# A planned graph-network kernel: cap turned by DMA, heads in twos, full products in layer three, GRU update on VectorE

## Chip, cores, metric

The kernel runs on one core of a Trainium2 chip. The metric is device time in microseconds of one launch. Engines are named as the profile names them: PE (TensorE matmuls), PEld (its weight loads), DVE (VectorE), ACT (ScalarE), POOL (GpSimd), SP (the queue that issues most DMAs).

## The reference

There are 64 graphs of 256 nodes with 256 features, `x`, and a 0/1 adjacency `adj`, which is about 1.6% full. Four layers follow one another; each takes h = relu(layernorm(x)) and adds its result to x.

- Layers 0 and 1: attention with 4 heads of 64. Scores e[i,j] = leaky_relu(src[i] + dst[j]) where there is an edge, softmax over j, product with the projected features Wh. (In layer 1 the edge types are 1 to 5, of which a 0/1 adjacency has type 1 alone.) Layer 0 ends in ELU; layer 1 adds a bias, relu, Wh, and a layer norm of each head.
- Layer 2: the same attention with one head of 256.
- Layer 3: three GRU steps. In each, m = h W_i, ag = A^T m, and

```
r = sigmoid(i_r + h_r);  z = sigmoid(i_z + h_z)
n = tanh(i_n + r * h_n)
h = (1 - z) * n + z * h
```

with i = ag w_ih^T + b_ih and h_* = h w_hh^T + b_hh.

## The kernel before

The work goes by pairs of graphs, 32 of them: a tile has 128 partitions, and `C` = 4 chunks of 128 nodes make the two graphs, `S` = 512 columns.

**The order.** A class `_Schedule` plans it while the program is built. Each piece of work is an `op` with an engine, a cost in ns, what it reads and writes, and the buffers that it takes. Due times are set backwards from `PACE` ns for each pair, with `STRETCH` times the cost and `MARGIN` between a piece and its user. Then a simulated clock runs, and each engine takes the enabled piece that is due first and has room in its buffers. The order found is laid down as the fixed order of every engine. Pieces of two or three neighbouring pairs thus interleave on each engine. Buffers are slots by name: 5 `xt`, 1 `at`, 3 `cap`, 1 `cap_n`, 3 `pt`, 9 `g`, 8 PSUM banks, and so on. An engine works in its order and waits where its next piece is not yet ready. The planner knows nothing of the chip beyond these costs.

**Softmax without a running maximum.** exp(leaky_relu(s + d)), up to a factor of the row, is the larger of two products of one column factor and one row factor. `factors` makes the factors: `f` (of the rows on partitions) by two ACT exponentials, and `cb`, the other factor repeated over all partitions. `cb` is made in one of two ways: for the first `SPREAD_PAIRS` = 2 pairs by broadcast matmuls (`spread`, L1075), later by a transpose (L1094), a small DMA to DRAM (`rd`) and a DMA that repeats it into SBUF. `weights` (L1128, then a minimum with `cap` on L823) gives the unnormalised weights `pt` on DVE: four `tensor_scalar` pieces and one `tensor_tensor`. `cap` is 2^120 where there is an edge, and 0 elsewhere; a row without any edge gets 2^-80 throughout.

**cap.** `layer0` loads `at` (the adjacency as int32). ACT takes a Square that checks that the values are 0 or 1 (L1191). DVE sums the degrees (L1197) and makes them 2^-80 or 0 (L1198). POOL casts `at` to bf16 `am`, and makes `cap_n` from it in four pieces (L1205). PE turns the eight 128x128 blocks (`turn`, L1218), and ACT copies them from PSUM to `cap`.

**attend.** A product of weights and features takes `pt` as the stationary operand in two halves of 64 columns:

```python
Q = P // 2
for jc in range(2):
    for q in range(2):
        i0 = ic * P + q * Q
        nc.tensor.matmul(ps[q * Q : (q + 1) * Q], lhsT=pt.tile[:, b, jc, i0 : i0 + Q], ...)
```

The profile shows these on L1148 as 128*64: 32 matmul records a head in layers 0 and 1 (65 columns, the last one the row sum), and 32 a pair in layer 2 (257 columns). `attend_head` does one head as one piece of PE work.

**GRU.** `gru` first splits h into a rounded part and the rest (`split`, `hl`), so that A^T h can be had in the faster fp32r form (`aggregate`, L1345). The W_i are folded into the input weights beforehand (`wc`). `gate` (L1359) makes the gate products in full fp32: 128x512, of `whh` with `ht` and of `wc` with `ag`. Each step has two units of 128 features; `unit` computes sigmoid as 0.5 (1 + tanh(v / 2)):

```python
d = ht - n                     # POOL
d = (z + 1) * d                # DVE, z is the tanh
h_new = 0.5 * d + n            # DVE
```

`rows_of` (L1373) turns h_new by PE for the next step, or for the sum onto `xt` at the end. A line L823 in the profile is the helper `vec`, through which most DVE, ACT and POOL pieces go; they are told apart by their tiles.

Of the kernel before, what the change touches and what calls it, by code (L numbers as in the profile page):

```python
# [518 lines left out]
SPREAD_PAIRS = 2  # L519
PACE = 97000.0  # L520
# [19 lines left out]
class _Schedule:  # L540
# [16 lines left out]
    STRETCH = 3.17  # L557
    MARGIN = 400.0
# [166 lines left out]
def _fast_path(  # L725
# [38 lines left out]
    P = 128  # L764
# [3 lines left out]
    NP = B // 2  # L768
# [16 lines left out]
    viol = consts.tile([P, NP + 1], F32, name="viol")  # L785
# [21 lines left out]
            "cb4_": (slots, 2), "cb1_": (slots, 1), "pt": (slots, 3), "o": (slots, 2),  # L807
# [106 lines left out]
    def check_columns():  # L914
# [4 lines left out]
        def norms():  # L919
# [12 lines left out]
        vec(nc.vector.tensor_scalar, 100, viol[:, NP : NP + 1], lambda: fit.tile[:, :1], -1.0, 1.0,  # L932
            op0=OP.mult, op1=OP.add, reads=[fit], writes=[(B_viol, NP)])
# [36 lines left out]
    def parts(b, keys):  # L970
        return [(b, k) for k in keys]

    def norm(xt, cls):

        st, mv = buf("st", [P, C, 6]), buf("mv", [P, 4, C])
        xn = buf(cls, [P, C, D])

        def stats(c):
            def emit():
                nc.vector.bn_stats(st.tile[:, c, :], xt.tile[:, c, :])  # L980
                nc.vector.bn_aggr(mv.tile[:, 0:2, c], st.tile[:, c, :])  # L981

            op("dve", 615, emit, [(xt, c)], [(st, c), (mv, c)])

        for c in range(C):
            stats(c)

        def power():
            nc.gpsimd.tensor_scalar(mv.tile[:, 2, :], mv.tile[:, 1, :], 1e-5, None, op0=OP.add)  # L989
            nc.gpsimd.tensor_tensor(mv.tile[:, 2, :], mv.tile[:, 2, :], nhalf[:, :C], op=OP.pow)  # L990

        op("pool", 1350, power, parts(mv, range(C)), [(mv, "r")])
        vec(nc.vector.scalar_tensor_tensor, 160, lambda: mv.tile[:, 3, :], lambda: mv.tile[:, 0, :], -1.0,
            lambda: mv.tile[:, 2, :], op0=OP.mult, op1=OP.mult,
            reads=parts(mv, range(C)) + [(mv, "r")], writes=[(mv, "b")])

        def apply(c):
            op("act", 610, lambda: nc.scalar.activation(  # L998
                xn.tile[:, c, :], xt.tile[:, c, :], AF.Relu,
                bias=mv.tile[:, 3, c : c + 1], scale=mv.tile[:, 2, c : c + 1],  # L1000
            ), [(xt, c), (mv, "r"), (mv, "b")], [(xn, c)])

        for c in range(C):
            apply(c)
        return xn

    def transposed(xn, cls):
        ht = buf(cls, [P, DC, S])

        def block(dc):  # L1010
            ps = bank()

            def emit():
                for c in range(C):
                    nc.tensor.transpose(  # L1015
                        ps.tile[:, c * P : (c + 1) * P], xn.tile[:, c, dc * P : (dc + 1) * P], ident
                    )

            op("pe", 445, emit, [xn], [ps], takes=[ht])
            vec(nc.scalar.copy, 600, lambda: ht.tile[:, dc, :], lambda: ps.tile,  # L1020
                reads=[ps], writes=[(ht, dc)], engine="act")

        for dc in range(DC):
            block(dc)
        return ht

    def project(ht, we, B_we, heads, width, shift):

        W = width + 2
        wh = buf("wh", [P, heads, C, W])  # L1030

        def rows(c):
            ps = bank()

            def emit():
                for dc in range(DC):
                    nc.tensor.matmul(  # L1037
                        ps.tile[:, : heads * W],
                        lhsT=ht.tile[:, dc, c * P : (c + 1) * P],
                        rhs=we[:, dc].rearrange("p h w -> p (h w)"),  # L1040
                        start=(dc == 0),
                        stop=(dc == DC - 1),
                    )

            op("pe", 895, emit, [ht, B_we], [ps], takes=[wh])

            def copy():
                src = ps.tile[:, : heads * W].rearrange("p (h w) -> p h w", h=heads)
                if shift:
                    nc.scalar.activation(wh.tile[:, :, c, :], src, AF.Identity, bias=shift)  # L1050
                else:
                    nc.scalar.copy(wh.tile[:, :, c, :], src)

            op("act", 390, copy, [ps], [(wh, c)])

        for c in range(C):
            rows(c)
        return wh

    def factors(wh, heads, width, slope, shift):  # L1060

        f = buf("f", [P, 2, heads, C])
        R = heads * C
        cb = buf(f"cb{heads}_", [P, heads, C, P])

        def spread(h):

            ps = bank()

            def emit():
                for c in range(C):
                    nc.tensor.matmul(  # L1075
                        ps.tile[:, c * P : (c + 1) * P],
                        lhsT=wh.tile[:, h, c, width + 1 : width + 2].to_broadcast([P, P]),
                        rhs=ident, start=True, stop=True,
                    )

            op("pe", 880, emit, [wh], [ps], takes=[cb])
            op("act", 700, lambda: nc.scalar.activation(
                cb.tile[:, h].rearrange("p c n -> p (c n)"), ps.tile, AF.Exp,
                scale=slope - 1.0, bias=-shift * (slope - 1.0),
            ), [ps], [(cb, h)])

        if sched.group < SPREAD_PAIRS:
            for h in range(heads):
                spread(h)
        else:  # L1090
            ps, row, rd = bank(), buf("row", [R, P]), buf("rd", [R, P])

            def emit_t():
                nc.tensor.transpose(  # L1094
                    ps.tile[:R, :P], wh.tile.rearrange("p h c w -> p (h c) w")[:, :, width + 1], ident
                )

            op("pe", 115, emit_t, [wh], [ps])

            def emit_row():  # L1100
                nc.scalar.activation(
                    row.tile, ps.tile[:R, :P], AF.Exp, scale=slope - 1.0, bias=-shift * (slope - 1.0)
                )

            op("act", 260, emit_row, [ps], [row])
            dma("act", 1 << 13, lambda: nc.scalar.dma_start(rd.tile, row.tile), [row], [rd])
            dma("sp", heads << 18, lambda: nc.sync.dma_start(
                cb.tile.rearrange("p h c n -> p (h c n)"),
                rd.tile.rearrange("(o r) n -> o (r n)", o=1).to_broadcast([P, R * P]),
            ), [rd], parts(cb, range(heads)))  # L1110

        def exps(k, a):
            op("act", 225, lambda: nc.scalar.activation(  # L1113
                f.tile[:, k], wh.tile[:, :, :, width], AF.Exp, scale=a, bias=-shift * a
            ), [wh], [(f, k)])

        exps(0, 1.0)
        exps(1, slope)
        op("pool", 150, lambda: nc.gpsimd.memset(wh.tile[:, :, :, width], 1.0), [], [wh])  # L1119
        return f, cb  # L1120

    def weights(cap, f, cb, h):

        pt = buf("pt", [P, 2, 2, N])

        def emit(b, jc):
            c = 2 * b + jc
            nc.vector.tensor_scalar(  # L1128
                pt.tile[:, b, jc, :].rearrange("p (i n) -> p i n", n=P),
                cb.tile[:, h, 2 * b : 2 * b + 2, :],  # L1130
                f.tile[:, 1, h, c : c + 1], f.tile[:, 0, h, c : c + 1], op0=OP.mult, op1=OP.max,
            )

        for b in range(2):
            for jc in range(2):
                op("dve", 425, lambda b=b, jc=jc: emit(b, jc), [(cb, h), f], [(pt, (b, jc))], port=True)
        vec(nc.vector.tensor_tensor, 1240, lambda: pt.tile, lambda: pt.tile, lambda: cap.tile, op=OP.min,
            reads=[cap], writes=[pt], port=True)
        return pt

    def attend(ps, pt, wh, c, h, w):
        b, ic = divmod(c, 2)

        Q = P // 2
        for jc in range(2):
            for q in range(2):
                i0 = ic * P + q * Q
                nc.tensor.matmul(  # L1148
                    ps[q * Q : (q + 1) * Q], lhsT=pt.tile[:, b, jc, i0 : i0 + Q],
                    rhs=wh.tile[:, h, 2 * b + jc, :w], start=(jc == 0), stop=(jc == 1),  # L1150
                )

    def attend_head(o, o_view, pt, wh, h):
        ps = bank()
        w = E + 1

        def emit():
            for c in range(C):
                attend(ps.tile[:, c * w : (c + 1) * w], pt, wh, c, h, w)
# [18 lines left out]
    def layer0(pair, p):  # L1178
# [31 lines left out]
        for c in range(C):  # L1210
            capped(c)
# [297 lines left out]
```

## Time and profile before

| | |
|---|---|
| time, median of 3 runs | 3250.36 us (3250.15 to 3252.92) |
| the profiled execution's own time | 3251.65 us |
| its span, first to last instruction | 3249.8 us |
| mean granted TensorE clock | 0.995 |
| gate matmuls, L1359 | 2304 of `whh` and 2304 of `wc`, 128x512 each |
| small head products, L1148, 128x65 | 8192 records, 274.2 us |
| POOL `g<-ht,g` (the d above) | 192, mean 1345 ns |
| DVE `g<-g,g` in the GRU | 384, mean 806 ns |
| DVE degree sums, L1197 | 32, mean 1200 ns |
| ACT copy of cap | 32, mean 1036 ns |

A row of the profile's list of groups has the line, engine and operation, the tiles (out<-in), shapes and count, then the sum of the busy times, the mean of one in ns, and the idle time of the engine just before them with what ended it. The durations of PE's rows overlap, since matmuls are pipelined: what one costs is read as the distance between starts. Shares of the span are averages; the first 200 us and the last 150 us look different from the middle.

### The profile page before, as it was taken

The page shows a single profiled execution, that of the slowest core. Times are in us where ns is not written, and L with a number is a line of the kernel's source. Part 1 is how long each engine was busy: PE and PEld are TensorE (multiplying, and loading weights), DVE is VectorE, ACT ScalarE, POOL GpSimd, SP SyncE. Part 2 cuts the span into 40 slices and gives each one's busy share as a digit, 9 for nine tenths or more (in the row PEclk, how much of TensorE's full clock was granted, in tenths as well). Part 3 has the DMA queues.
Part 4 walks back from the last instruction along what each step waited for, and adds up shares of the span by engine and source line. Part 5 has one row for each costly group of instructions (what it writes and reads, how often), then busy time and mean ns, then how long its engine had stood idle before and what let it go on. Part 6 is the DMA issues. An engine that isn't in the chain of part 4 may idle for free.

```text
span 3249.8 us, 49723 instructions
## 1 busy us (share of the span) xinstructions
PE 3189.6 (98%) x19256; PEld 1901.5 (59%) x19256; DVE 2463.4 (76%) x4965; ACT 1468.8 (45%) x2847; POOL 1131.6 (35%) x1108
## 2 busy tenths in 40 slices
PE   7799999999999999999999999999999999999998
PEld 6556556556656566555565555565565666565554
DVE  8867777787787777787777787877877877777742
ACT  4444444444444444444444444444444454444432
POOL 3532343442343423334332333423434233333220
PEclk9899999999999999999999999999999999999999
DMA  3101111111101101111011111111011011010000
GB/s 100 40 20 43 43 30 46 43 37 43 56 30 40 40 33 56 30 46 43 24 56 43 43 43 34 37 43 56 30 46 42 25 56 40 30 47 21 30 10 14
DMA packets 72549, 129.28 MB, mean 40 GB/s; under 512 B 7736, under 2 KB 60400, under 8 KB 64624
## 3 DMA queue, kind: packets, MB, share of 16 engines
q1 hardware_dynamic: 68368, 124.66, 11.7%
q8 instruction: 154, 2.52, 0.3%
q10 hardware_dynamic: 3936, 1.35, 0.2%
q14 instruction: 91, 0.75, 0.1%
HBM read 108.66 MB, written 17.33 MB: 39 GB/s over the span
## 4 chain that ended last, share of the span: by engine, by line
PE 90%; DVE 7%; POOL 2%; ACT 0%; issue 0%; DMA 0%; ACTq 0%; POOLq 0%; DVEq 0%
PE bank L1359 57%; PE bank L1148 11%; PE bank L1037 10%; PE bank L1345 5%; PE bank L1015 3%; PE bank L1373 2%; DVE pt L1128 2%; DVE st L980 1%; POOL cap_n L1205 1%; DVE mv L981 1%; DVE pt L823 1%; DVE xt L823 0%; PE bank L943 0%; PE bank L1075 0%; DVE mv L823 0%
## 5 line engine op out<-in xcount | busy, mean ns | idle before, releaser
L1359 PE MATMUL bank<-ht,whh 128*128 128x512 f32 x2304 | 1069.0, 596 | 0.4 <-ACT ht L823 0.3
L1359 PE MATMUL bank<-ag,wc 128*128 128x512 f32 x2304 | 1063.0, 594 | 0.0
L1359 PEld LDWEIGHTS bank<-ag,wc 128*128 128x128 f32 x2304 | 424.5, 190 | 482.0 <-issue 476.7
L1359 PEld LDWEIGHTS bank<-ht,whh 128*128 128x128 f32 x2304 | 421.3, 190 | 471.4 <-issue 430.2
L823 ACT ACTIVATE g<-bank,bg 128x512 f32<-128x512 f32 x576 | 393.7, 686 | 573.5 <-PE bank L1359 549.6
L823 DVE SCALAR_TENSOR_TENSOR g<-g,g 128x512 f32<-128x512 f32 x384 | 308.4, 806 | 427.9 <-ACT g L823 424.3
L1128 DVE TENSOR_SCALAR pt<-cb,f 128x256 f32<-128x256 f32 x1152 | 463.4, 470 | 11.0 <-PE bank L1148 8.1
L1148 PEld LDWEIGHTS bank<-wh,pt 128*64 128x64 f32 x9216 | 324.3, 137 | 136.9 <-issue 67.7
L1148 PE MATMUL bank<-wh,pt 128*64 128x65 f32 x9216 | 392.2, 241 | 10.3 <-DVE pt L823 10.3
L823 POOL TENSOR_TENSOR g<-ht,g 128x512 f32<-128x512 f32 x192 | 257.0, 1345 | 290.0 <-ACT g L823 289.9
L823 DVE TENSOR_TENSOR pt<-pt,cap 128x1024 f32<-128x1024 f32 x288 | 354.9, 1267 | 1.0
L989 POOL TENSOR_SCALAR mv<-mv 128x4 f32<-128x4 f32 x128 | 49.4, 386 | 698.2 <-DVE mv L981 634.7
L823 ACT COPY ag<-bank 128x512 f32<-128x512 f32 x192 | 112.3, 585 | 313.1 <-PE bank L1345 312.4
L823 ACT ACTIVATE g<-g,bg 128x512 f32<-128x512 f32 x192 | 137.8, 718 | 230.8 <-DVE g L823 225.1
L998 ACT ACTIVATE xn<-xt,mv 128x256 f32<-128x256 f32 x384 | 203.8, 590 | 67.3 <-DVE mv L823 67.3
L1345 PE MATMUL bank<-am_r,hl 128*128 128x256 f32 x1536 | 218.3, 295 | 0.0
L980 DVE BATCH_NORM_STATS2 st<-xt 128x6 f32<-128x256 f32 x512 | 208.6, 407 | 7.9 <-DMA xt<-in_x_dram 6.8
L1345 PEld LDWEIGHTS bank<-am_r,hl 128*128 128x128 f32 x1536 | 190.7, 188 | 31.7 <-issue 20.3
L823 DVE TENSOR_TENSOR g<-g,bank 128x512 f32<-128x512 f32 x192 | 131.0, 683 | 91.7 <-PE bank L1359 91.7
L1119 POOL MEMSET wh<- 128x16 f32 (+1 forms) x96 | 11.6, 121 | 518.0 <-ACT f L1113 518.0
L823 ACT COPY ht<-bank 128x512 f32<-128x512 f32 x256 | 141.2, 597 | 84.1 <-PE bank L1015 84.1
L823 POOL TENSOR_TENSOR o<-o,bias_b 128x512 f32<-128x512 f32 x64 | 101.2, 1583 | 210.7 <-DVE o L823 208.7
(94 smaller groups left out, 3686.8 us busy)
## 6 DMA issues: line engine op xcount, KB each, us to landing
cb<-rd SPq DMA_DIRECT2D x60, 1024.0 KB, 4.8
xt<-in_x_dram SPq DMA_DIRECT2D x32, 512.0 KB, 4.8
at<-in_adj_dram SPq DMA_DIRECT2D x32, 512.0 KB, 3.8
out_dram<-xt SPq DMA_DIRECT2D x32, 512.0 KB, 5.6
cb<-rd SPq DMA_DIRECT2D x30, 256.0 KB, 3.9
rd<-row ACTq DMA_DIRECT2D x60, 8.0 KB, 1.4
whh<-in_L_gnn_w_hh_dram SPq DMA_DIRECT2D x1, 768.0 KB, 6.4
g<-in_L_gnn_weight_dram SPq DMA_DIRECT2D x3, 256.0 KB
```

The costliest lines, as they stand in the source:

```text
L823: emit = lambda: fn(*[a() if callable(a) else a for a in args], **kw)
L980: nc.vector.bn_stats(st.tile[:, c, :], xt.tile[:, c, :])
L981: nc.vector.bn_aggr(mv.tile[:, 0:2, c], st.tile[:, c, :])
L989: nc.gpsimd.tensor_scalar(mv.tile[:, 2, :], mv.tile[:, 1, :], 1e-5, None, op0=OP.add)
L998: op("act", 610, lambda: nc.scalar.activation(xn.tile[:, c, :], xt.tile[:, c, :], AF.Relu, bias=mv.tile[:, 3, c : c + 1], scale=mv.tile[:, ...
L1015: nc.tensor.transpose(ps.tile[:, c * P : (c + 1) * P], xn.tile[:, c, dc * P : (dc + 1) * P], ident)
L1037: nc.tensor.matmul(ps.tile[:, : heads * W], lhsT=ht.tile[:, dc, c * P : (c + 1) * P], rhs=we[:, dc].rearrange("p h w -> p (h w)"), start=( ...
L1128: nc.vector.tensor_scalar(pt.tile[:, b, jc, :].rearrange("p (i n) -> p i n", n=P), cb.tile[:, h, 2 * b : 2 * b + 2, :], f.tile[:, 1, h, c ...
L1148: nc.tensor.matmul(ps[q * Q : (q + 1) * Q], lhsT=pt.tile[:, b, jc, i0 : i0 + Q], rhs=wh.tile[:, h, 2 * b + jc, :w], start=(jc == 0), stop= ...
L1345: nc.tensor.matmul(ps.tile[:, b * N : (b + 1) * N], lhsT=hl.tile[:, k, 2 * b + sc, :], rhs=am.tile[:, 2 * b + sc, :], start=(k == 0 and sc ...
L1359: nc.tensor.matmul(ps.tile, lhsT=w[:, dc, g * P : (g + 1) * P], rhs=v.tile[:, dc, :], start=(first and dc == 0), stop=(last and dc == DC - 1),
L1373: nc.tensor.transpose(ps.tile[:, c * P : (c + 1) * P], ht.tile[:, j, c * P : (c + 1) * P], ident)
```

## The change

1. `turn` becomes a DMA on SP with `transpose=True`, one for each of the four chunks of `cap_n`, straight into `cap`. The eight PE transposes, their PSUM bank and the ACT copy are gone.
2. The degrees come from ACT: four Identity activations over 256 columns, which write `am` and accumulate the row sum. DVE's reduction and POOL's cast are gone.
3. `attend_heads` does two heads as one piece of PE work in two banks; `pt` has 4 slots.
4. `attend` takes the width Q of a stationary block. Layer 2 has Q = 128, full products; the heads keep 64.
5. The GRU update: d = (z + 1) * h, n = (z - 1) * n, and h_new = d - n, which is twice the new state; steps 2 and 3 take a scale of 0.25 in place of 0.5 to undo it. All three pieces are on DVE, and the POOL piece is gone. The addition of the input part of n becomes a `scalar_tensor_tensor` with a factor, and so does the last sum onto `xt`.
6. `SPREAD` is 1 for 2, `PACE` 100000 for 97000, `STRETCH` 3.46 for 3.17, `MARGIN` 800 for 400.
7. All functions move into `graphs(u, first, nb)`, which could also take a single graph (`nb` = 1); here all 32 units have nb = 2, so that costs and shapes are those of before.

```diff
-SPREAD_PAIRS = 2
-PACE = 97000.0
+SPREAD = 1
+PACE = 100000.0
...
-    STRETCH = 3.17
-    MARGIN = 400.0
+    STRETCH = 3.46
+    MARGIN = 800.0
...
-            "cb4_": (slots, 2), "cb1_": (slots, 1), "pt": (slots, 3), "o": (slots, 2),
+            "cb4_": (slots, 2), "cb1_": (slots, 1), "pt": (slots, 4), "o": (slots, 2),
...
+        def attend(ps, pt, wh, c, h, w, Q):
+            b, ic = divmod(c, 2)
+            for jc in range(2):
+                for q in range(P // Q):
+                    i0 = ic * P + q * Q
...
+        def attend_heads(o, o_view, pts, wh, hs):
+            banks_ = [bank() for _ in hs]
+            w = E + 1
+            def emit():
+                for ps, pt, h in zip(banks_, pts, hs):
+                    for c in range(C):
+                        attend(ps.tile[:, c * w : (c + 1) * w], pt, wh, c, h, w, P // 2)
+            op("pe", pe(944) * len(hs) + 90, emit, [*pts, wh], banks_, takes=[o])
...
+            for k in range(0, H, 2):
+                hs = (k, k + 1)
+                attend_heads(o, o_view, [weights(cap, f, cb, h) for h in hs], wh, hs)
...
-            nc.vector.tensor_reduce(deg.tile, at.tile, AX.X, OP.add)
-        vec(nc.gpsimd.tensor_copy, 1080, lambda: am.tile, lambda: at.tile, reads=[at], writes=[am],
-            engine="pool", port=True)
+            def degree(c):
+                op("act", 560, lambda: nc.scalar.activation(
+                    am.tile[:, c, :], at.tile[:, c, :], AF.Identity, accum_out=deg.tile[:, c : c + 1]
+                ), [at], [(am, c), (deg, c)])
...
-                        nc.tensor.transpose(
-                            ps.tile[:, (2 * b + jc) * N + ic * P :][:, :P],
-                            cap_n.tile[:, 2 * b + ic, jc * P : (jc + 1) * P],
-                            ident_h,
-                        )
...
-        vec(nc.scalar.copy, 1040, lambda: cap.tile.rearrange("p b j n -> p (b j n)"), lambda: ps.tile,
-            reads=[ps], writes=[cap], engine="act")
+            def turn(c):
+                b, ic = divmod(c, 2)
+                dma("sp", 1 << 16, lambda: nc.sync.dma_start(
+                    cap.tile[:, b, :, ic * P : (ic + 1) * P], cap_n.tile[:, c, :], transpose=True
+                ), [(cap_n, c)], [(cap, c)])
...
-            op("pe", 910, lambda: attend(ps.tile[:, : D + 1], pt, wh, c, 0, D + 1), [pt, wh], [ps])
+                op("pe", 870, lambda: attend(ps.tile[:, : D + 1], pt, wh, c, 0, D + 1, P), [pt, wh], [ps])
...
-                vec(nc.gpsimd.tensor_tensor, 1290, lambda: d.tile, lambda: ht.tile[:, j, :],
-                    lambda: n.tile, op=OP.subtract, reads=[(ht, j), n], writes=[d], engine="pool", port=True)
...
-                vec(stt, 700, lambda: d.tile, lambda: z.tile, 1.0, lambda: d.tile,
-                    op0=OP.add, op1=OP.mult, reads=[z], writes=[d], port=True)
-                vec(stt, 700, lambda: h_new.tile[:, j, :], lambda: d.tile, 0.5, lambda: n.tile,
-                    op0=OP.mult, op1=OP.add, reads=[d, n], writes=[(h_new, j)], port=True)
+                    vec(stt, dve(700), lambda: d.tile, lambda: z.tile, 1.0, lambda: ht.tile[:, j, :],
+                        op0=OP.add, op1=OP.mult, reads=[z, (ht, j)], writes=[d], port=True)
+                    vec(stt, dve(700), lambda: n.tile, lambda: z.tile, -1.0, lambda: n.tile,
+                        op0=OP.add, op1=OP.mult, reads=[z], writes=[n], port=True)
+                    vec(stt, dve(700), lambda: h_new.tile[:, j, :], lambda: d.tile, 2 * half, lambda: n.tile,
+                        op0=OP.mult, op1=OP.subtract, reads=[d, n], writes=[(h_new, j)], port=True)
```

## The prediction, made before the result was known

> **What bounds the kernel now.** The first reading is the busy line of the page with its span, and then the same by stretches, taken for 1000 to 2000 us, which no start or end touches. The columns of the second answer are the length of the stretch, then busy time and instructions of each engine, TensorE's granted clock, and DMA.
>
> ```profile
> span 3249.8 us, 49723 instructions
> PE 3189.6 (98%) x19256; PEld 1901.5 (59%) x19256; DVE 2463.4 (76%) x4965; ACT 1468.8 (45%) x2847; POOL 1131.6 (35%) x1108
> ```
> ```profile
> 1000.00:2000.00 1000.00, 996.65 (x6123) 592.90 (x6122) 784.81 (x1564) 458.43 (x888) 357.67 (x344) 1.00 0.12 41
> ```
>
> In steady state PE, the matmul engine, is busy 996.65 of 1000 us at full clock, and the chain that ended last lies to 90% on PE. DVE stands at 78%. So a microsecond taken off PE's own work is a microsecond of the kernel, as long as what feeds PE stays early. Whether it is early is told by PE's waits (total us, times, longest):
>
> ```profile
> PE bank L1015 <- ACT xn L998: 23.7, 3, 13.7
> PE bank L1148 <- DVE pt L823: 10.3, 14, 2.3
> PE bank L1373 <- DVE ht L823: 6.6, 8, 1.5
> PE bank L1218 <- POOL cap_n L1205: 3.3, 15, 0.3
> ```
>
> These are nearly all waits of PE, about 55 us, and 23.7 of them are three waits at the start. The price of each PE piece is the distance from its start to the start of the next piece, in PE's timeline of one pair (start, length, line, shapes, count); the lengths overlap, so they are not added.
>
> ```profile
> 647.69 0.61 PE L1218 MATMUL bank<-ident_h,cap_n 128*128 128x128 bf16 x8
> 648.13 1.04 PE L1015 MATMUL bank<-ident,xn 128*128 128x128 f32 x8
> ...
> 651.16 3.71 PE L1037 MATMUL bank<-w2e,ht 128*128 128x258 f32 x16
> 654.71 0.60 PE L1373 MATMUL bank<-ident,ht 128*128 128x128 f32 x4
> 655.14 1.88 PE L1359 MATMUL bank<-ht,whh 128*128 128x512 f32 x4
> 656.96 3.03 PE L1148 MATMUL bank<-wh,pt 128*64 128x65 f32 x96
> 659.91 2.16 PE L1345 MATMUL bank<-am_r,hl 128*128 128x256 f32 x16
> 661.91 1.88 PE L1359 MATMUL bank<-ht,whh 128*128 128x512 f32 x4
> 663.72 1.15 PE L1148 MATMUL bank<-wh,pt 128*64 128x65 f32 x32
> 664.80 1.98 PE L1359 MATMUL bank<-ht,whh 128*128 128x512 f32 x4
> ...
> 689.41 3.69 PE L1148 MATMUL bank<-wh,pt 128*64 128x257 f32 x32
> 693.04 2.16 PE L1345 MATMUL bank<-am_r,hl 128*128 128x256 f32 x16
> ```
>
> The eight turns of cap cost 648.13 - 647.69 = 0.44 us. A lone head (x32) costs 1.08 us, three in a row (x96) 2.95, so a further head in a run costs (2.95 - 1.08)/2 = 0.935: the run itself costs 0.145. The gate pair ahead of a head lasts 1.81 (661.91 to 663.72) where it lasts 1.72 ahead of its like. Each run of heads thus costs 0.145 + 0.09 = 0.24 us beyond its products.
>
> [...] the GRU's `g<-g,g` takes 806 ns on the mean, but 0.69 us in the last 70 us, where POOL is nearly idle.
>
> **PE's part of the change.** Counts are from the changed program's instruction order, costs from above.
> - Cap by DMA: 256 PE turns go, 32 x 0.44 = 14.1 us, and the waits for cap_n, 3.3 us: -17.4.
> - Heads in twos: the order before has 144 unbroken runs of head products, the changed one 97 (66 of two heads, 31 of four). 47 x 0.24 = -11.3.
> - Third layer: 32 matmuls in 128*64 form, 693.04 - 689.41 = 3.63 plus 0.09 ahead, become 16 of 128x257 in full form. Nearest row: 16 of 128x258 on L1037, 3.55. 32 pairs x 0.17 = -5.4.
> - SPREAD 1 for 2 pairs: 36 broadcast matmuls at 0.115 us (32 take 3.67 early in the trace) for 3 transposes of 0.11: -3.8.
>
> Sum -37.9 us, bounds -33 (halved gain for runs) to -44 (third layer at 0.26, other short waits for cap gone). The gates (2304 + 2304 matmuls) and all else on PE stay.
>
> **What is added elsewhere, and its cover.**
> - DVE: POOL's 192 subtractions leave; each unit gets one more scalar_tensor_tensor, 192 x 0.69 to 0.81 = +132 to +155; 32 reductions of 1.20 leave (-38). DVE goes from 77 us of a pair's 98.4 to about 80.5 of 97, 83%. PE covers it: zero, at worst the PE waits on DVE above (17 us) half as long again, +8.
> - POOL: 192 x 1345 ns and 32 casts of 1085 ns leave, -292: 1132 to 840. Not on the path; it may give DVE back some of the 0.12 us a piece[...]. I count nothing.
> - ACT: four degree passes a pair, each a 256-wide activation (0.39 to 0.59) plus a read of the accumulator (0.22), less the cap copy (1.04): +1.4 to +2.2 us a pair, 46 to 48 us of 97. Covered by PE. At the start two passes now stand ahead of the ht copies, and two with the Square ahead of the wh copies: up to 2 us later there, while the cap copy (1.01 us) ahead of cb goes. I count 0, range -3 to +8 for the whole start.
> - SP: 128 DMA transposes of 64 KB, two 128x128 blocks each: [...] at least 1.4 (landing of the small rd DMA). Each waits on SP for its POOL cap_n. Queued behind them are the next `at`, an output and the cb of layer 0; at the start, whh and the GRU weights. cap_n is made nearly a pair period ahead, and cap is first read by DVE after norm, turn, project and cb: at the start 18 us from loaded xt (about 7) to the first pt (25.07). Hidden in the middle: zero.
> - The later path in a unit. Before, POOL's d was ready before z, and after tanh(z) came two DVE pieces. Now three come after it (d, n, h_new). With no other work (3186 to 3190 us) the two turns of h_new started at 3188.28 and 3189.89; with a piece of 0.69 more each, and the second unit's pieces queued behind the first's on DVE, they start 0.69 and about 1.06 us later. Five such ends lie bare in the last 150 us, some half covered: +4 us, range +2 to +6. In steady state others' gates cover it; if the cover goes, each unit costs up to 1.06.
> - pt 4 slots for 3, and PACE, STRETCH and MARGIN, which only shift the planner's priorities: no instruction; their effect is in the order counted.
>
> **Sum.** Span 3249.8 - 37.9 + 4 = 3216. The profiled execution took 3251.65, 1.3 above the median 3250.36; from the median: 3250.4 - 34 = 3216 us.
>
> **Rivals.**
> 1. PE sheds, the rest stays hidden (above): 3216, 3200 to 3232 by the bounds. For it: PE at 99.7% with only short waits. Chance 0.70.
> 2. Half of it is lost again: [...] (more than 18 us for four eats the slack, +8), and a two-head product waits for its second weights (97 runs, 0.1 us each, +10): 3234, 3228 to 3243. For it: 14 waits on pt already, and both heads needed before PE begins. Against: 4 pt slots. 0.11.
> 3. The cover is lost in full: the gain equals the loss. That is also the case in which the order differs but the prices (0.24 a run) do not shrink with it. 3250; 0.06.
> 4. Slower, by one mechanism: DVE's lengthened end of the unit stands bare before L1373's turn of h_new in steady state too, because a DVE at 83% in a fixed order has other pieces ahead. Price 1.06 us a unit, 192 units; it decides from 34/1.06 = 32 bare units on. With half bare, 96 x 1.06 = 102 - 34: 3318; with a third, 3284, which I take. For it: DVE is the next busiest. Against: only 8 turns waited for DVE before. 0.13.
>
> That the change does not do what it says is excluded by the order for PE's counts; only the transposes' speed is unknown.
>
> **How the numbers follow.** A measurement of this kernel tells 0.2%, 6.5 us, from no change. Cases 1 and 2 end below 3243.9: 0.81 faster. Case 3 is 0.06 same, case 4 0.13 slower. The range 3199 to 3250 takes cases 1 and 2 and half of 3, and leaves case 4 and the outer ends out.
>
> **What would show it.** Right: no L1218 group on PE; L1148's small products in about 97 runs; PE busy still over 99% of 1000:2000; POOL near 840, DVE near 2560 or a little less; the turn of h_new waiting some 2 us a layer on DVE only after 3050. Wrong: PE's waits on DVE (pt, ht) at tens of us in the middle would be case 4; waits of DVE's pt for the cap DMA, case 2.

## Result and profile after

| | before | after |
|---|---|---|
| median | 3250.79 us (12 runs) | 3249.03 us (12 runs, 3247.32 to 3252.52) |
| ratio, 95% interval | | 0.9995 (0.9986 to 1.0004) |
| span of the profiled execution | 3249.8 us | 3245.5 us |

No difference that can be told from none, where 34 us less was forecast. The work did leave PE, and PE is no longer what the end hangs on. The profile page of the changed kernel gives its span, busy line and the shares of the chain that ended last; then comes the stretch from 1000 to 2000 us (length, then busy time and instructions of PE, PEld, DVE, ACT and POOL, granted clock, DMA share, GB/s):

```profile
span 3245.5 us, 48064 instructions
...
PE 3156.9 (97%) x18419; PEld 1908.1 (59%) x18419; DVE 2348.1 (72%) x5125; ACT 1457.5 (45%) x3065; POOL 818.5 (25%) x884
...
PE 74%; DVE 22%; POOL 2%; issue 1%; ACT 0%; DMA 0%; POOLq 0%; ACTq 0%; DVEq 0%
```
```profile
1000.00:2000.00 1000.00, 989.96 (x5880) 597.02 (x5879) 746.66 (x1623) 459.13 (x972) 263.81 (x276) 1.00 0.14 43
```

PE's busy time in the middle fell from 996.65 to 989.96 of 1000 us, and the chain lies to 22% on DVE. Before, it was 90% PE and 7% DVE:

```profile
PE 90%; DVE 7%; POOL 2%; ACT 0%; issue 0%; DMA 0%; ACTq 0%; POOLq 0%; DVEq 0%
```

The work per pair fell, and idle time came in its place. The waits of PE (us in total, times, longest) show where:

```profile
PE bank L1032 <- ACT xn L1015: 37.6, 4, 17.0
PE bank L1361 <- DVE g L829: 16.8, 28, 0.6
PE bank L1389 <- DVE ht L829: 8.1, 6, 1.8
PE bank L1361 <- DVE am_r L829: 6.4, 28, 0.2
```

The waits for `cap_n` are gone, and of those for `pt` one of 0.4 us is left. New are two on L1361, the aggregation, 28 times each: once a pair, at one place. The first line belongs to the start. Now that place on the three engines. VectorE's timeline (start, length, line, tiles, shapes, count, and in brackets the idle time before with what ended it):

```profile
1085.41 0.69 DVE L829 TENSOR_TENSOR hl<-bank,hl 128x512 fp32r<-128x512 f32 x1 [0.87 <-ACT hl L1346]
...
1097.16 7.43 DVE L1145 TENSOR_SCALAR pt<-cb,f 128x256 f32<-128x256 f32 x16
1104.52 0.68 DVE L829 SCALAR_TENSOR_TENSOR o<-mean,o 128x512 f32<-128x512 f32 x1
1105.12 4.62 DVE L829 TENSOR_TENSOR pt<-pt,cap 128x1024 f32<-128x1024 f32 x4
...
1112.45 0.66 DVE L829 CAST am_r<-am 128x1024 fp32r<-128x1024 bf16 x1
1113.03 1.29 DVE L829 SCALAR_TENSOR_TENSOR g<-g,g 128x512 f32<-128x512 f32 x2
1114.24 0.68 DVE L829 SCALAR_TENSOR_TENSOR g<-bank,g 128x512 f32<-128x512 f32 x1
```

PE's and POOL's timelines of the same time:

```profile
1108.99 3.95 PE L1163 MATMUL bank<-wh,pt 128*64 128x65 f32 x128
1113.17 1.21 PE L1361 MATMUL bank<-am_r,hl 128*128 128x256 f32 x8 [0.23 <-DVE am_r L829]
1114.97 1.21 PE L1361 MATMUL bank<-am_r,hl 128*128 128x256 f32 x8 [0.60 <-DVE g L829]
1116.28 3.67 PE L1375 MATMUL bank<-ht,whh 128*128 128x512 f32 x8
```
```profile
1100.01 2.82 POOL L829 TENSOR_TENSOR hl<-hn,hl 128x512 fp32r<-128x512 f32 x2 [3.56 <-ACT hl L1346]
```

From 1085.41 to 1113.03 VectorE has hardly a gap (the longest is 0.33 us): after the turn of h_new (PE, at 1083.95) come the scaling of heads, layer 2's rows, statistics, then all 16 `pt` pieces and four minima for the four heads of the next pair, and only then the cast `am_r` and the `g<-bank,g` that empties a bank. PE needs both for the aggregation. This is a loop: PE's turn of h_new, 28 us of VectorE, PE's aggregation. The 16 `pt` pieces take 7.43 us, though a piece follows another after 0.32 to 0.33. Two of them, started at 1100.07 and 1101.49, last 1.49 us each: the two in which POOL subtracts.

The kernel before has such a stretch too, here from 690.55 to 715.29, with 12 and 4 `pt` pieces and two long ones among them:

```profile
695.52 0.66 DVE L823 CAST am_r<-am 128x1024 fp32r<-128x1024 bf16 x1
698.34 5.05 DVE L1128 TENSOR_SCALAR pt<-cb,f 128x256 f32<-128x256 f32 x12
706.72 2.33 DVE L1128 TENSOR_SCALAR pt<-cb,f 128x256 f32<-128x256 f32 x4
715.29 0.69 DVE L823 TENSOR_TENSOR g<-g,bank 128x512 f32<-128x512 f32 x1 [0.41 <-PE bank L1359]
```

But there the cast `am_r` stands ahead of the `pt` pieces, 20.9 us before the aggregation that needs it (716.42), and at 715.29 it is VectorE that waits for PE. In the changed order the cast stands behind them, 0.7 us before the aggregation.

The period is read as the distance between the starts of layer 2's products of successive pairs. Over 22 pairs in the middle its mean was 98.47 us before (99.35 and 97.60 in turn) and 98.33 after (most of them 98.30).

### The profile page after: what moved, and what is told of

Its sections match the earlier page's. It is cut to its first block, busy times and chain, and to the rows that moved or that the text cites. A ratio compares the mean times of both kernels' runs of the same rounds, so it can differ in the third digit from the quotient of the medians.

```text
span 3245.5 us, 48064 instructions
## 1 busy us (share of the span) xinstructions
PE 3156.9 (97%) x18419; PEld 1908.1 (59%) x18419; DVE 2348.1 (72%) x5125; ACT 1457.5 (45%) x3065; POOL 818.5 (25%) x884
## 4 chain that ended last, share of the span: by engine, by line
PE 74%; DVE 22%; POOL 2%; issue 1%; ACT 0%; DMA 0%; POOLq 0%; ACTq 0%; DVEq 0%
PE bank L1375 46%; PE bank L1054 10%; PE bank L1163 7%; DVE pt L1145 7%; DVE pt L829 4%; PE bank L1361 4%; PE bank L1032 3%; PE bank L1389 3%; DVE st L997 2%; DVE g L829 2%; DVE mean L829 2%; POOL mv L1007 2%; DVE o L829 2%; DVE xt L829 1%; DVE mv L998 1%
## 5 line engine op out<-in xcount | busy, mean ns | idle before, releaser
L1375 PE MATMUL bank<-ht,whh 128*128 128x512 f32 x2304 | 1057.9, 596 | 5.4 <-ACT g L829 1.5
L1375 PE MATMUL bank<-ag,wc 128*128 128x512 f32 x2304 | 1049.0, 593 | 0.0
L1375 PEld LDWEIGHTS bank<-ag,wc 128*128 128x128 f32 x2304 | 428.1, 190 | 524.0 <-issue 496.1
L1375 PEld LDWEIGHTS bank<-ht,whh 128*128 128x128 f32 x2304 | 425.8, 190 | 494.4 <-issue 443.3
L829 ACT ACTIVATE g<-bank,bg 128x512 f32<-128x512 f32 x576 | 390.0, 682 | 330.5 <-PE bank L1375 316.9
L829 DVE SCALAR_TENSOR_TENSOR g<-g,g 128x512 f32<-128x512 f32 x384 | 289.3, 760 | 157.7 <-ACT g L829 155.4
L1163 PE MATMUL bank<-wh,pt 128*64 128x65 f32 x8704 | 377.2, 232 | 2.8 <-POOL mv L1006 1.3
L829 ACT ACTIVATE g<-g,bg 128x512 f32<-128x512 f32 x192 | 138.4, 721 | 532.1 <-DVE g L829 529.2
L1163 PEld LDWEIGHTS bank<-wh,pt 128*64 128x64 f32 x8704 | 341.6, 141 | 55.9 <-issue 39.7
L829 DVE TENSOR_TENSOR pt<-pt,cap 128x1024 f32<-128x1024 f32 x288 | 337.2, 1215 | 0.0
L1361 PE MATMUL bank<-am_r,hl 128*128 128x256 f32 x1536 | 238.8, 299 | 23.2 <-DVE g L829 16.8
L829 DVE SCALAR_TENSOR_TENSOR g<-g,ht 128x512 f32<-128x512 f32 x192 | 144.5, 753 | 117.9 <-ACT g L829 117.9
L1361 PEld LDWEIGHTS bank<-am_r,hl 128*128 128x128 f32 x1536 | 199.2, 189 | 44.2 <-DVE g L829 22.5
L829 ACT COPY ag<-bank 128x512 f32<-128x512 f32 x192 | 112.0, 583 | 207.1 <-PE bank L1361 203.3
L829 DVE SCALAR_TENSOR_TENSOR g<-bank,g 128x512 f32<-128x512 f32 x192 | 131.0, 682 | 88.5 <-PE bank L1375 88.5
L1069 ACT COPY wh<-bank 128x264 f32<-128x264 f32 (+1 forms) x256 | 97.2, 394 | 165.4 <-PE bank L1054 165.3
L1007 POOL TENSOR_TENSOR mv<-mv,nhalf 128x4 f32<-128x4 f32 x128 | 166.9, 1304 | 10.7
L1006 POOL TENSOR_SCALAR mv<-mv 128x4 f32<-128x4 f32 x128 | 63.5, 496 | 347.9 <-DVE mv L998 199.8
```

The costliest lines, as they stand in the source:

```text
L829: emit = lambda: fn(*[a() if callable(a) else a for a in args], **kw)
L1361: nc.tensor.matmul(ps.tile[:, b * N : (b + 1) * N], lhsT=hl.tile[:, k, 2 * b + sc, :], rhs=am.tile[:, 2 * b + sc, :], start=(k == 0 and sc ...
L1375: nc.tensor.matmul(ps.tile[:, :S], lhsT=w[:, dc, g * P : (g + 1) * P], rhs=v.tile[:, dc, :], start=(first and dc == 0), stop=(last and dc ...
```

## Experiments

Three theories at first. **A**: VectorE's stretch before the aggregation sets the pace. **B**: VectorE waits 262 us in all for `cb` (shown under e3), and that holds it up. **C**: PE is the bound as before, and its pieces have become slower. Ratios are to the kernel before.

**1. e1_hl_thin: the subtraction off POOL.**

```diff
+                if engine == "pool":
+                    vec(nc.gpsimd.memset, cost, lambda: hl.tile[:, 1].bitcast(F32), 0.0, ...)
+                    return hl
                 vec(fn, cost, lambda: hl.tile[:, 1], src, lambda: hl.tile[:, 0], op=OP.subtract, ...)
```

> The changed kernel, same order on every engine; in the first layer of the GRU POOL writes zeros into hl's second half instead of subtracting (the low part of the split of hn is left out). Theory A (loop through VectorE): from the turn of h_new to the first aggregation of the next graph pair VectorE works without a gap (1085.4 to 1113.0 us), and 2.1 us of it are two pt pieces that take 1.41 instead of 0.33 us while POOL subtracts (1100.0 to 1102.8). With the subtraction gone the pieces are short, am_r and the freed bank come in time, PE's waits on L1361 (16.8 + 6.4 us) go, and the period falls by 0.7 to 1.0 us: 3249 - 22 to 30 = 3219 to 3227. Theory B (the wait of pt for cb, 262 us, sets the pace): no change, 3249. Theory C (PE is bound by its own work, its pieces became slower): no change, 3249.

Measured 3196.17 us, 0.9830 (0.9816 to 0.9843). VectorE's line in the same place, the chain, and 1000 to 2000 us:

```profile
1083.14 5.26 DVE L1145 TENSOR_SCALAR pt<-cb,f 128x256 f32<-128x256 f32 x16
```
```profile
PE 97%; DVE 2%; ACT 0%; DMA 0%; POOL 0%; issue 0%; ACTq 0%; DVEq 0%; POOLq 0%
```
```profile
1000.00:2000.00 1000.00, 1000.00 (x5907) 608.34 (x5902) 731.33 (x1652) 472.01 (x991) 252.77 (x286) 1.00 0.14 44
```

The 16 pieces lost 2.17 us, PE is busy without a gap from 1000 to 2000 us, and the period is 96.47 us. A holds, B and C fall. The gain is twice what A had put down, 53 us for 22 to 30. A had counted PE's listed waits and the slow step after them, 0.7 to 1.0 us a pair. By the records, a pair's aggregations got 1.09 us shorter, its gates 0.47 and its heads 0.30: the last two in hesitations of about 0.1 us, which no line of waits lists.

**2. e2_cast_act: the cast on ACT.**

```diff
-            vec(nc.vector.tensor_copy, dve(700), lambda: am.tile, lambda: am_h.tile, ..., port=True)
+            vec(nc.scalar.copy, act(1050), lambda: am.tile, lambda: am_h.tile, ..., engine="act")
```

> The changed kernel with the cast am_r<-am issued on ACT, planned at 1050 ns, instead of VectorE. Theory A: VectorE's gapless stretch before the first aggregation is 0.6 us shorter and the aggregation no longer waits for am_r; the bank's release comes 0.6 us earlier: -0.5 to -0.8 us a pair, 3249 - 15 to 25 = 3224 to 3234. Theory B: no change, 3249. Theory C: no change, 3249, with PE's waits on L1361 gone and as much lost in other places.

3238.78 us, 0.9962 (0.9948 to 0.9975). PE's waits on L1361 are gone; `PE bank L1163 <- DVE g L829: 27.3, 28, 1.2` came in their place: the order, planned anew, has a head product where the late bank is wanted. A's sign, with a third less than its lower end.

**3. e3_cb_free: cb without its wait.**

```diff
-                    rd.tile.rearrange(...).to_broadcast([P, R * P]),
+                    x[0, : R * P // D, :].rearrange(...).to_broadcast([P, R * P]),
```

> The changed kernel, same order; the broadcast load of cb reads the first rows of x in place of rd, so that it waits for no row of scores (the scores of the source nodes are left out of cb, after the first pair). Theory B: pt's 262 us of waiting for cb go, VectorE is up to 9 us a pair earlier, and with it PE: -20 to -30 us, 3219 to 3229. Theory A: VectorE's waits move to the next pieces that need PE (ACT's g at 1065.3, the slot of pt at 1083.0), the gapless stretch begins where PE lets it; within 0.2% in the middle, at most some 5 us from the start: 3244 to 3249. Theory C: the same as A.

3250.92 us, 0.9997 (0.9989 to 1.0005). The wait for `cb`, in the changed kernel

```profile
DVE pt L1145 <- DMA cb<-rd: 262.2, 29, 11.3
```

left the list, and `DVE g L829 <- ACT g L829` grew from 273.2 to 520.0 us. A wait of 262 us was worth nothing: B is out.

**4. e4_turn_twice: more work for PE.**

```diff
-  for c in range(C):
+  for c in (*range(C), *range(C if cls == "ht3_" else 0)):
       nc.tensor.transpose(...)
```

> The changed kernel, same order; the eight turns of hn into ht3_ are done twice on PE, 0.86 us more of PE work in each pair, lying between the turn of h_new and the first aggregation of the next pair. Theory A: PE has 0.8 us of waiting at the end of that stretch, which the added work fills: 0 to +6 us, 3249 to 3255. Theory C (PE's own work is the bound): 32 x 0.86 = +27, 3276. Theory B: as A, 3249, if the cb chain stands outside the stretch.

3249.24 us, 0.9998 (0.9990 to 1.0006). PE took 0.87 us a pair more for nothing; the wait on L1361 for `g` shrank, and the one for `am_r` is gone:

```profile
PE bank L1361 <- DVE g L829: 5.6, 28, 0.2
```

So at this place, once in each pair, the changed kernel is not bound by PE. If that is so, less work on PE can't help it either.

**5. g1_thin_plus4 and g2_thin_plus7: VectorE's stretch made longer.** Both are e1 with `pt` pieces of layer 0 issued twice, which changes no value.

```diff
+            more = {2: 4}.get(h, 0) if B_now[0] == 0 else 0        # g2: {2: 4, 3: 3}; B_now is 0 in layer 0
+            def emits(b, jc):
+                for _ in range(2 if 2 * b + jc < more else 1):
+                    emit(b, jc)
...
-                    op("dve", 425, lambda b=b, jc=jc: emit(b, jc), ...)
+                    op("dve", 425, lambda b=b, jc=jc: emits(b, jc), ...)
```

> e1_hl_thin, same order, with four pt pieces of the third head in the first layer issued twice on VectorE, 4 x 0.325 = 1.30 us a pair in the stretch ahead of the first aggregation. Theory A (the length of VectorE's stretch sets the pace once it exceeds PE's work beside it; e1 took 2.17 us out and gained 1.83 a pair, so 0.34 was to spare): +0.96 a pair, x 28 = +27, 3223. Rival (POOL's subtraction itself, or a late hl, was what held PE, not the time that VectorE lost): 3196 to 3200. Rival (VectorE's busy total): 1.3 x 32 over 3200 us is nothing, 3196.

> As g1 with seven pieces twice (third and fourth head), 7 x 0.325 = 2.28 us a pair, about what VectorE lost to POOL in the changed kernel. Theory A: 2.28 - 0.34 = 1.94 a pair, x 28 = +54, 3250, and PE's waits on L1361 for am_r and g are back. Rivals: 3196 to 3200.

Measured 3238.13 us, 0.9957 (0.9943 to 0.9970), and 3279.24 us, 1.0083 (1.0069 to 1.0097): more than A's sizes (3223 and 3250). A piece issued twice onto the same tile took 0.445 us, not 0.325. The pieces of the stretch in g1 and in g2:

```profile
1095.23 7.04 DVE L1147 TENSOR_SCALAR pt<-cb,f 128x256 f32<-128x256 f32 x20
```
```profile
1110.38 8.39 DVE L1147 TENSOR_SCALAR pt<-cb,f 128x256 f32<-128x256 f32 x23
```

In g2 both waits of the aggregation are back, as forecast (L1375 is its line there):

```profile
PE bank L1375 <- DVE g L829: 16.7, 28, 0.6
PE bank L1375 <- DVE am_r L829: 6.9, 29, 0.5
```

With these lengths the four kernels of this order lie on a line:

| kernel | `pt` pieces of the stretch | beyond e1 | period | beyond e1 |
|---|---|---|---|---|
| e1_hl_thin | 5.26 us | | 96.47 us | |
| g1_thin_plus4 | 7.04 | 1.78 | 97.87 | 1.40 |
| after | 7.43 | 2.17 | 98.30 | 1.83 |
| g2_thin_plus7 | 8.39 | 3.13 | 99.22 | 2.75 |

From 0.34 to 0.38 us are free, and then each microsecond of the stretch is a microsecond of every pair. g1 and g2 have no subtraction on POOL, so what counts is the time that VectorE loses, not what POOL does.

**6. f2_split_dve: the subtraction on VectorE, nothing left out.**

```diff
-                aggregate(ag, split(lambda dc=dc: hn.tile[...], "pool", [hn]), dc)
+                aggregate(ag, split(lambda dc=dc: hn.tile[...], "dve", [hn]), dc)
```

> The changed kernel with the subtraction of hn's split planned on VectorE instead of POOL, computation complete. Theory A: VectorE gets 2 x 0.66 us more a pair, and two pt pieces lose the 2.17 us that they stand waiting while POOL subtracts: its stretch is 0.85 us shorter if the two stay in it, -0.85 x 29 = -25, 3224; if they fall outside it, up to the 53 us of e1_hl_thin, 3196. A theory in which VectorE's total busy time counts gives +1.3 x 32 = +42 or no change.

3198.87 us, 0.9843 (0.9829 to 0.9856): faster than both kernels, by one word. VectorE got more to do, and the end hangs on PE again:

```profile
PE 96%; DVE 2%; POOL 0%; ACT 0%; DMA 0%; issue 0%; ACTq 0%; POOLq 0%; DVEq 0%
```
```profile
1000.00:2000.00 1000.00, 1000.00 (x5934) 607.46 (x5933) 753.82 (x1677) 470.27 (x978) 235.21 (x267) 1.00 0.14 44
```

VectorE is busy 753.82 of 1000 us here, 746.66 in the changed kernel that is 50 us slower. Its share of busy time told nothing; its place did. But two things changed at once, since the order was planned anew: no `pt` piece is held by a subtraction any more (the 16 pieces take 5.25 us from 1180.10), and the cast `am_r` moved ahead of them (1179.50, 8.1 us before its aggregation at 1187.64). What each of the two is worth was not tested; e1, with the order kept, is the clean comparison.

**7. f1_before_thin, h1_before_full, h2_before_twice: was the kernel before bound by PE?** f1 is the edit of e1, h2 that of e4, and h1 puts Q = 128 into layer 2, each alone on the kernel before, same order.

> The kernel before, same order, with POOL's subtraction of hl in the first layer of the GRU replaced by zeros (the low part of the split of hn is left out), as e1_hl_thin did to the changed kernel (3196). Theory P (PE's prices in the prediction were right, and in both kernels VectorE's stretch with two pt pieces held up by POOL took the difference): PE's own work is 34 to 38 us more here than in e1_hl_thin: 3230 to 3234. Theory Q (the kernel before was bound by PE alone, so nothing is to be had there): 3250. Theory R (the prices were wrong, the change takes little off PE): 3196 to 3205.

> The kernel before, same order, with the third layer's products in full form (16 of 128x257 a pair in place of 32 in 128*64 form): one part of the change alone. If PE's own work is the bound: by the prediction -5.4, by f3_thin_halves (+9.4 for the way back) -9, 3242. If the kernel before is held by another chain as the changed one is: 3251, no change.

> The kernel before, same order, with the eight turns of hn done twice (0.86 us of PE a pair), as e4_turn_twice did to the changed kernel (no change there). If PE's own work is the bound: 32 x 0.86 = +27, 3278. If it is held by another chain with PE waiting in small pieces: 3251 to 3260.

| | time | ratio (95%) |
|---|---|---|
| f1_before_thin | 3249.39 us | 0.9994 (0.9986 to 1.0003) |
| h1_before_full | 3244.15 us | 0.9978 (0.9969 to 0.9987) |
| h2_before_twice | 3282.42 us | 1.0098 (1.0082 to 1.0113) |

It was. Work added to PE shows in full (+31.7 us for 28 of turns), work taken off shows in part (-6.5 us, where the records of the two forms differ by 0.34 us a pair, 11 in all), and f1 gains nothing that is clear of noise, so theory Q holds, against my P. Yet the same collision is in the trace of the kernel before, in the pieces of over 0.8 us that its `pt` row hides in a mean: 62 of them, which last 65 us longer in all than the usual 0.41 us each. The changed kernel has 59, and 64 us. The loss is not new: what changed is what stands behind it. f1, in which POOL writes zeros at that place, does not take all of it away: VectorE is busy 2426.2 us in it, 37.2 less than the 2463.4 before, not 65 less. There VectorE had time to spare, as at 715.29 above.

**8. f3_thin_halves, f4_thin_single, g4_cap_pe: what the parts are worth on PE.** f3 is e1 with layer 2 in halves, in the same order; f4 is e1 with single heads, and g4 is f2 with cap turned by PE and copied by ACT, both planned anew.

```diff
 f3 -  attend(ps..., 0, D + 1, P)          f4 -  for k in range(0, H, 2): hs = (k, k + 1)
    +  attend(ps..., 0, D + 1, P // 2)        +  for k in range(H): hs = (k,)      # PACE = 97000
 g4 -  nc.sync.dma_start(cap..., cap_n..., transpose=True)
    +  nc.tensor.transpose(ps..., cap_n..., ident_h)   # 8 a pair, then nc.scalar.copy to cap
```

> e1_hl_thin (3196, PE busy 1000 of 1000 us) with the third layer's products in 64-column halves again, same order. There PE is the bound, so the price of this part shows: by the prediction 32 x 0.17 = +5.4 us, by the spacing of the two kernels' records (3.63 + 0.09 against 3.29 us) 32 x 0.34 to 0.43 = +11 to 14: 3201 to 3210. If PE were not the bound: 3196.

> e1_hl_thin with the heads issued one by one and PACE 97000 (the planner's order for single heads at PACE 100000 leaves PE gaps). By the prediction 0.24 us for each of some 47 more runs, +11: 3207. If a run costs nothing beyond its products: 3196. If the new order leaves waits of its own, more than 3215, with PE's waits showing them.

> f2_split_dve (3199, PE busy 1000 of 1000 us) with cap turned by PE into a bank and copied by ACT again, in place of the four transposes by DMA; order planned anew. By the prediction 14.1 us of turns and 3.3 of waits: 3213 to 3216. By the records of the two kernels (0.64 us a pair): 3219. [...] If the new order leaves waits, PE's waits show them.

- f3: 3205.56 us, 9.4 more than e1 (0.32 us a pair in the period, 96.79 against 96.47).
- g4: 3223.30 us, 24.4 more than f2; its turns take 0.447 us a pair, 14.3 us. In its chain VectorE has 21% again, so the other 10 us may be VectorE's and are not cap's price.
- f4: 3257.87 us, 62 more than e1. Its order has 124 runs of heads in place of 97, and brought waits of its own, so that the price of a run could not be had:

```profile
PE bank L1379 <- DVE g L829: 40.7, 27, 1.5
```

**9. g3_old_planning: the changed kernel with the planner's old values.**

```diff
-PACE = 100000.0
+PACE = 97000.0
...
-    STRETCH = 3.46
-    MARGIN = 800.0
+    STRETCH = 3.17
+    MARGIN = 400.0
```

> The changed kernel with PACE 97000, STRETCH 3.17 and MARGIN 400 of the kernel before. If the order is what decides (theory A), the period changes by more than 0.3 us a pair either way: below 3240 if the two pt pieces no longer stand before an aggregation, above 3260 if more pieces do. If the parameters are idle: 3249.

3261.69 us, 1.0030 (1.0018 to 1.0043). These three numbers issue no instruction and are worth 12.7 us: the order decides. Its trace has 109 `pt` pieces of over 0.8 us, where the changed kernel has 59. But the mean period rose by 0.23 us only (98.53), less than the 0.3 expected; what the rest of the 12.7 us is made of stays open.

## Why the prediction was wrong, step by step

**What bounds the kernel (PE): right.** h2 and h1 show it. But it was true of the order before, and the change lays down another.

**PE's sum, -37.9: right in sign, too small.** Without VectorE's hold the change is worth 3249.4 - 3196.2 = 53 us (f1 against e1; an estimate, as f1 keeps a part of the hold). Terms:
- Third layer, -5.4: h1 shows -6.5 and f3 +9.4 for the way back. The records of the two kernels differ by 0.34 us a pair (3.625 and 3.285), 10.9 us in all, so my nearest row, L1037 with 0.17, was a poor stand-in.
- Cap, -17.4: eight turns in a row were priced well (0.44 against 0.447 in g4). In the kernel before they took 0.45 us in one pair and 0.83 in the next, waits included: 20.5 us.
- SPREAD, -3.8: counted as 36 broadcast matmuls, but each leaves two records and the price of 0.115 us was that of a record. 72 fewer (144 before, 72 after), less the three transposes, make -7.9.
- Heads in twos, -11.3: not settled by a run (f4). The records of the head products are 8.24 us a pair with single heads (h1) and 7.92 in e1: 10 us, near the price (estimate).

By these records the terms come to some 50 of the 53 us. The third layer, SPREAD and cap were sized too small.

**"DVE goes from 77 us of a pair's 98.4 to about 80.5 of 97, 83%. PE covers it: zero": this step failed, and with it the forecast.** It was argued from VectorE's share and from waits of 17 us in the old order. The cover is not a share; it is the time between two things that PE does, the turn of h_new and the next aggregation, against the VectorE work that must lie between them in the fixed order. In the new order that work is 27.6 us, and 2.17 of it is waiting for POOL. Without these 2.17 us the same order takes 1.83 us a pair less, 53 us in all (e1): the term put at zero took the whole gain. What the new order did is seen in the traces: the cast `am_r` went from ahead of the `pt` pieces to behind them, and the head products that need these pieces now stand in one run of 128 right ahead of the aggregation, where 64, 32 and 32 stood between gates before. The cast alone is not all of it, since its removal gains 10 us (e2). Which of the edits brought this order was not tested.

**POOL beside VectorE, "some of the 0.12 us a piece" and "I count nothing": the wrong reading of a mean.** It is not a small tax on each piece, but a full stop for a few. The stop is in the trace of the changed kernel: 57 `pt` pieces (one SBUF tensor in, f32) start while POOL's subtraction runs; all of them end 0.15 us after it, and the one that starts 0.06 us after POOL's lasts 1.49 us in place of 0.41. What makes them stop is not shown. Nor does every GpSimd instruction stop such a piece: in the kernel before, 38 `pt` pieces started inside POOL's `mv<-mv,nhalf` (128x4, 1.04 us) and lasted 0.38 to 0.41 as always. The prediction took up only `g<-g,g`, which has two SBUF inputs.

**DVE at 2560: 2348.1.** The instructions were as counted (+160). With POOL's 192 subtractions and 32 casts gone, pieces that overlap POOL cost some 120 us beyond the usual in place of 290 (estimate, each form's excess over its median without POOL).

**Hidden transposes: right.** No wait on a DMA for `cap` is in the list. SP issues four in

```profile
1087.31 5.56 SPq L1240 DMA_TRANSPOSE cap<-cap_n  x4
```

and is held 1.24 us by each at the median (the profile shows no time to landing for these).

**The tail and the start: right in kind.** In the last 100 us the first turn of a layer end waits 1.26 to 1.27 us (0.68 to 0.78 before), and the second 1.21 and 1.29 in the first two ends (0.92 to 0.96): some 0.5 and 0.3 more, where 0.69 and 1.06 had been put down. The start cost 5.4 us up to the seventh pair's layer 2 (694.76 against 689.41), inside its range.

**The planner's values, "no instruction": true, and not the point.** Their effect, said to be in the order counted, is not in PE's counts but in who stands behind whom (g3).

**Rivals.** The number was rival 3's, the cover lost in full, to which I gave 0.06. The mechanism was rival 4's, VectorE with other pieces ahead in a fixed order, at another place (the aggregation, not the turn of h_new), and with the loss stopping at the size of the gain by chance: in g2, which has no subtraction on POOL, a `pt` stretch 1 us longer than the changed kernel's ended at 3279. So it is luck that 3249 lies inside the stated range, near its upper end of 3250. The signs named beforehand did not warn either: the counts came true (97 runs of heads, POOL at 818.5), PE stayed at 99.0% from 1000 to 2000 us, and the waits watched for were those on `pt` and `ht`, where `am_r` and a bank's release came. Of rival 2's waits for transposes there is no sign, and the wait for a DMA that is there, 262 us for `cb`, is worth nothing (e3).

## What to carry to other kernels

Before counting work off the busiest engine as time, find the loop: take two pieces of that engine between which another engine must finish something, and add up what the other engine does between them in the new order. Read the long pieces of a row as well as its mean, since here the stop shows as a few pieces of three to four times the length. And a wait of 262 us in all can lie off the path, while two of 0.2 and 0.6 us a pair mark it.

## What the runs showed of the hardware

- A VectorE `tensor_scalar` f32 with one SBUF input stood still for the whole of a GpSimd subtraction: 1.49 to 1.51 us for 0.41, in 57 cases of 57 in the changed kernel. A GpSimd piece on 128x4 did not hold it up (38 pieces of the kernel before, 0.41 us at most).
- The same piece issued again onto the tile just written costs 0.445 us (g1) where distinct tiles follow at 0.325 (e1).
- On POOL the subtraction of 128x512 took 1.41 us and cost VectorE 1.08 besides; on VectorE it takes 0.69 (f2).
- An aggregation product of 128x256, with `hl` and `am_r` written as fp32r, follows another after 0.117 us at the median in the kernel before; a gate product of 128x512 in full fp32 after 0.429, which is 0.215 for 256 columns.
- A DMA transpose of a 128x256 bf16 chunk holds SP for 1.24 us at the median; how long it takes to land no run here shows.
